# Feature attentions: maxima and values leave their PSUM bank through ScalarE, one subtraction on GpSimd, a bias folded into another

## The chip, the cores and the metric

The kernel runs on one core of one Trainium2 chip. The metric is the device time of one execution in microseconds (us), the median of several runs. PE is the matrix engine (PEld its weight loads), DVE the vector engine, ACT the scalar engine, POOL GpSimd, SP the engine that issues most DMAs; "ACTq" and "SPq" in a timeline are DMA issues of those engines' queues.

## What is computed

A chain of eight residual blocks on x (32 x 64 x 256) with a context of the same size; between them stand layer norms. The blocks are called A to H in the kernel. The change touches the two "feature attentions", A and E, in which the positions of the attention are the 256 features and the 64 rows of a sample are split in heads of 8:

```python
# A: q = layernorm(x), k = v = ctx, each (32, 64, 256): 8 heads of 8 rows, 256 queries and keys
qk = jnp.einsum('bhdq,bhdl->bhql', qh, kh) * scale
sm = jax.nn.softmax(qk, axis=-1)
ret = jnp.einsum('bhql,bhdl->bhdq', sm, vh)
x = x + gamma * ret

# E: the same on layernorm(x) with projections over the 64 rows and a band of +-64 features
qkv = x @ w_in.T + b_in
q, k, v = jnp.split(qkv, 3, axis=-1)
scores = jnp.where(band, q @ k / sqrt(8), -inf)
attn = jax.nn.softmax(scores, axis=-1)
o = attn @ v
o = o @ w_out.T + b_out
out = (relu(o).T * ctx) projected by w_ct, + b_ct
```

B, D, F and H are feed-forward blocks (D with an attention of its own and experts, H with experts), C an attention over tokens, G an attention with a sigmoid.

## The kernel before

The 2048 rows are 16 tiles of 128 rows (two samples each). Stages A to H run one after the other; each stage loads the next one's weights. In A and E all 16 tiles go through one software pipeline, `attention_slots`, in which the order of every instruction is written out by hand: time is cut in slots t, a tile takes eight slots, and tile i meets its steps at fixed offsets from 8i. Steps of several tiles share a slot. The steps, with their offsets:

- `prepare` (-2 to 9): layer norm, q (in E the projections, L1139 and L1141: qp and kp on PE, fq and fk on ACT), then `stacks`: q and k are each split on POOL into three bfloat16 terms (t3q, t3k: L194 to L198), written to DRAM by SP (d3q, d3k) and loaded again as stacked rows (stq, stk, 192 KB each, L211).
- `score_maxima` (16 to 26): 16 score products of a tile (L242; in E with the band added first, L238), two a slot; DVE takes the negated maxima (negm, L246). At offset 24 PE transposes them (nmT, L250); they too are split in three bfloat16 terms: the first on ACT (nm, L253), the remainder on DVE (nmr, L256), the second and third on POOL (L257, L258). At offset 26 three DMAs of ACT's queue (L261) put the terms as three more rows into stq, so that the scores of the next step come out with the maximum taken off.
- `values` (23): transposed values in PSUM (cT in A, vp in E, L1165), copied by DVE into vmo (L441; in E L1168, where the values' bias is added).
- `attend_unit` (30 to 37): score products with the keys on partitions (L273), exponent on ACT (e, L277), in E the band cut out by POOL (L285).
- `product_unit` (32 to 39): values times exponents into o (L295), two slots after their unit.
- `finish` (40 to 52): oc copied from o by ACT (L356), the denominators by two products (den, L306), copied by ACT (rd, L308), reciprocals on DVE (L312), num, and in E two more projections (o2 at L1178, o3 at L1185; y on ACT adds b_out at L1180).

In slot 24 of a tile PE does: the first half of a unit's scores (L273), one score product of the next tile (L242), nmT, the second half (L273), the product o, the second L242; slot 25 begins with den of the tile before. DVE's order there is negm, the two vmo copies, negm, negm, nmr, ACT's is e, oc, nm, e, rd, e, the three DMA issues, and in E fq.

Each engine runs its instructions in the order in which they were written. The PSUM tiles cT, vp, nmT, den, qp, kp, o2 and o3 carry the tag "tp", for which there is one buffer: whoever comes next in PE's order waits until the last reader of the one before is done. For nmT that last reader is nmr on DVE (it reads `src`, the transposed maxima), for cT and vp the second vmo copy. The score tiles s1 and s2 and the work pools have two buffers each, o has one, e four.

`load_E` issues the DMAs of E's weights during stage D; `first_of_E` runs E's constants and the first tiles' operands beside D's last products.

Of the kernel before, what the change touches and what calls it, by code (L numbers as in the profile page):

```python
# [9 lines left out]
F32 = mybir.dt.float32  # L10
# [3 lines left out]
ALU = mybir.AluOpType  # L14
# [3 lines left out]
P = 128  # L18
T = 2048
D = 256  # L20
# [11 lines left out]
def tile_net(ctx: ExitStack, tc: tile.TileContext, a: dict, out: bass.AP):  # L32
    nc = tc.nc
    V, S, G, PE = nc.vector, nc.scalar, nc.gpsimd, nc.tensor
# [9 lines left out]
    def fetch(i):  # L44
        nc.sync.dma_start(xs[i], a["x"][i * P : (i + 1) * P, :])
        nc.sync.dma_start(cs[i], a["ctx_2048"][i * P : (i + 1) * P, :])
# [53 lines left out]
    def bcast_row(pool, src, n, name):  # L100
        t = pool.tile([P, n], F32, name=name)
        nc.sync.dma_start(t, src.partition_broadcast(P) if len(src.shape) == 1 else src.to_broadcast([P, n]))
        return t
# [78 lines left out]
    def values_of(vmo, lc):  # L182

        return vmo[:, lc].rearrange("p c (q z) -> p c q z", z=40)[:, :, :, 0:8]
# [38 lines left out]
    def banded(band):  # L223
        return [(0, 192), (64, 256)] if band is not None else [(0, D), (0, D)]

    def score_maxima(pool, psum, k, qs, ks, band, i):

        qr = banded(band)
        negm = pool.tile([P, 2, 16], F32, name="negm")
        for qc in range(2):
            lo, hi = qr[qc]
            for hp in range(8):
                sc = psum.tile([P, 2, D], F32, tag="s1", name=f"s1_{i}_{qc}_{hp}", bufs=2)
                if band is not None:
                    PE.matmul(  # L238
                        sc[:, :, lo:hi], identb, band[:, qc, :, lo:hi], start=True, stop=False, skip_group_check=True,
                    )  # L240
                for hh in range(2):
                    PE.matmul(  # L242
                        sc[:, hh, lo:hi], qs[0:96, 2 * hp + hh, qc * P : (qc + 1) * P], ks[0:96, 2 * hp + hh, lo:hi],
                        start=band is None, stop=True, skip_group_check=band is not None,
                    )
                V.tensor_reduce(negm[:, qc, 2 * hp : 2 * hp + 2], sc[:, :, lo:hi], AX.X, ALU.max, negate=True)  # L246
                yield
        tp = psum.tile([P, 2, P], F32, tag="tp", name=f"nmT_{i}")
        for qc in range(2):
            PE.transpose(tp[0:16, qc, :], negm[:, qc, :], ident)  # L250
        src = tp[0:16].rearrange("h c t -> h (c t)")
        nm3 = pool.tile([16, 3, D], BF, name="nm3")
        S.copy(nm3[:, 0, :], src)  # L253
        yield
        r = pool.tile([16, D], F32, name="nmr")
        V.tensor_tensor(r, src, nm3[:, 0, :], ALU.subtract)  # L256
        G.tensor_copy(nm3[:, 1, :], r)  # L257
        G.tensor_tensor(nm3[:, 2, :], r, nm3[:, 1, :], ALU.subtract)  # L258
        yield
        for t in range(3):  # L260
            nc.scalar.dma_start(qs[96 + t : 97 + t], nm3[:, t, :])  # L261
        yield
# [139 lines left out]
    def run_A(w, side):  # L402
        with ExitStack() as es:
            cp = es.enter_context(tc.tile_pool(name="Ac", bufs=1, side=side))
            pool = es.enter_context(tc.tile_pool(name="Aw", bufs=2, side=side))
            dram = es.enter_context(tc.tile_pool(name="Ad", bufs=4, space=bass.MemoryType.DRAM))
            psum = es.enter_context(tc.tile_pool(name="Ap", bufs=1, space=PSUM))
            k = {}
            parts = attention_constants(cp, k)
            masks = []  # L410

            def prepare(i):
                if i + AHEAD < NT:
                    fetch(i + AHEAD)
                if i == 3:
                    pending.pop()()
                mv, rstd = ln_stats(pool, [xs[i]])
                V.tensor_scalar(mv[:, :, 0], mv[:, :, 0], -1.0, None, ALU.mult)
                yield
                q = pool.tile([P, D], F32, name="q")  # L420
                G.tensor_scalar(q, xs[i], mv[:, 0, 0:1], rstd, ALU.add, ALU.mult)
                if i < 4:
                    operand_buffers(cp, k, i)
                yield
                yield
                yield
                yield from stacks(pool, k, dram, q, cs[i], i)

            def start(t):
                if t in (16, 18):  # L430
                    next(parts)
                if t == 20:
                    for r in range(2):
                        masks.append(cp.tile([P, 1], F32, name=f"gmask{r}"))
                        V.tensor_tensor(masks[r], k["mask"][r], w["gamma"], ALU.mult)

            def values(i):
                tp = transpose_to(psum, cs[i], "tp", f"cT_{i}")
                yield
                for lc in range(2):  # L440
                    V.tensor_copy(  # L441
                        values_of(k["vmo"][i % 2], lc), tp[:, lc, :].rearrange("p (c q d) -> p c q d", c=4, q=4)
                    )
                yield

            def finish(i, oc):

                rd = yield from normalised(pool, psum, k, oc, i, 4, masks)
                G.tensor_tensor(xs[i], xs[i], rd, ALU.add)
                yield  # L450

            attention_slots(pool, psum, k, None, SCALE8, prepare, values, finish, start)


# [633 lines left out]
    def load_E(wp):  # L1088
        w = {}
        w["band"] = load(wp, [P, 2, D], a["c_band"], "band")  # L1090
        for nm in ("b_in", "b_out", "b_ct"):
            w[nm] = load(wp, [P, 3 if nm == "b_in" else 1], a[f"L2_xattn_{nm}"], nm)
        w["bv"] = bcast_row(wp, a["L2_xattn_bv"], P, "ebv")
        bd = wp.tile([P, 5, P], F32, name="bd")
        G.memset(bd, 0.0)
        for h0 in (0, 64):
            rows = slice(h0, h0 + 64)
            nc.sync.dma_start(
                bd[rows, 0:3, h0 : h0 + 64], a["L2_xattn_w_in"].rearrange("i (t o) -> i t o", t=3)
            )  # L1100
            nc.sync.dma_start(bd[rows, 3, h0 : h0 + 64], a["L2_xattn_w_out"])
            nc.sync.dma_start(bd[rows, 4, h0 : h0 + 64], a["L2_xattn_w_ct"])
        w["bd"] = bd

        between.append(lambda psum: first_of_E(w, psum))
        return w
# [3 lines left out]
    def first_of_E(w, psum):  # L1110

        w["k"], w["cstack"], w["normed"] = {}, ExitStack(), {}
        side = side_of("E")
        cp = w["cstack"].enter_context(tc.tile_pool(name="Ec", bufs=1, side=side))
        for b in range(4):
            operand_buffers(cp, w["k"], b)
            yield
        yield from attention_constants(cp, w["k"])
        w["bandb"] = cp.tile([P, 2, 2, D], BF, name="bandb")
        V.tensor_copy(w["bandb"], bc(w["band"], 2, [P, 2, 2, D]))  # L1120
        w["dram"] = w["cstack"].enter_context(tc.tile_pool(name="Ed", bufs=4, space=bass.MemoryType.DRAM))
        yield
        xp = w["cstack"].enter_context(tc.tile_pool(name="Ex", bufs=4, side=side))
        w["xp"] = xp
        yield
        with tc.tile_pool(name="Ef", bufs=1, side=side) as pool:
            for i in range(EARLY):
                yield from operands_of_E(w, pool, psum, i)
# [17 lines left out]
    def run_E(w, side):  # L1146
        bd = w["bd"]
        with ExitStack() as es:
# [5 lines left out]
            pool = es.enter_context(tc.tile_pool(name="Ew", bufs=2, side=side))  # L1154
            psum = es.enter_context(tc.tile_pool(name="Ep", bufs=1, space=PSUM))
            k, band, st = w["k"], w["bandb"], w["normed"]
# [4 lines left out]
            def values(i):  # L1161
                xn = st[i]
                vp = psum.tile([P, 2, P], F32, tag="tp", name=f"vp_{i}")
                for lc in range(2):
                    PE.matmul(vp[:, lc, :], xn[:, lc * P : (lc + 1) * P], bd[:, 2, :], start=True, stop=True)  # L1165
                yield
                for lc in range(2):
                    V.tensor_tensor(  # L1168
                        values_of(k["vmo"][i % 2], lc), vp[:, lc, :].rearrange("p (c q d) -> p c q d", c=4, q=4),
                        w["bv"].rearrange("p (c q d) -> p c q d", c=4, q=4), ALU.add,  # L1170
                    )
                yield

            def finish(i, oc):
# [472 lines left out]
```

## Time and profile before

| | us |
|---|---|
| median of 3 runs | 2920.18 |
| the runs | 2913.55 to 2922.21 |
| the profiled execution | 2917.11 |
| its span, first to last instruction | 2915.4 |

| engine | busy us | share |
|---|---|---|
| PE | 2455.6 | 84% |
| DVE | 1932.7 | 66% |
| ACT | 1513.6 | 52% |
| POOL | 1485.2 | 51% |

The mean granted TensorE clock was 0.962. Stage A ends at about 325 us, stage E stands between about 2057 and 2380 us. Durations of single instructions of the steps concerned (median, ns): vmo copy 281 in A and in E, nm on ACT 362, nmr on DVE 402, the second and third term on POOL 387 and 660, oc 580, rd 372.

How to read the lines below: a timeline line has start and length in us, the engine, the line of the kernel, the instruction, what it writes <- what it reads, the shape and the count of merged instructions; in brackets the idle time of the engine just before it and what ended it. A line of waits has the waiting engine and tile, the one waited for, us in total, times, and the longest.

### The profile page before, as it was taken

What the parts mean: (1) busy time and instruction counts of PE and PEld (TensorE: products, weight loads), DVE (VectorE), ACT (ScalarE), POOL (GpSimd) and SP (SyncE); (2) the same over time, 40 slices, a digit from 0 to 9 for tenths busy, and PEclk for the clock granted to TensorE, in tenths of its full rate; (3) what the DMA queues carried; (4) which work ended last, traced back from release to release, by engine and by line L of the source; (5) the groups of instructions that cost most, each with busy time, mean ns of one, the idle gap of its engine ahead of it and who ended that gap; (6) DMA issues with size and microseconds to landing.
All of it is one profiled execution on the core that took longest, in us unless ns stands there. A gap on an engine that the chain in (4) does not pass through costs nothing.

```text
span 2915.4 us, 44332 instructions
## 1 busy us (share of the span) xinstructions
PE 2455.6 (84%) x15966; PEld 1452.3 (50%) x16070; DVE 1932.7 (66%) x4084; ACT 1513.6 (52%) x2049; POOL 1485.2 (51%) x1649
## 2 busy tenths in 40 slices
PE   4888698777777777679999999789888876789999
PEld 2444344344444444446666666556555533445555
DVE  7777655599999999765545555663667659843322
ACT  1555421399999999745555555353244446521111
POOL 4554433388888888765555555311577754400000
PEclk9999899899999999989999999889999988899999
DMA  6543000399999999920000000000433300200000
GB/s 165 116 105 88 23 1 1 60 203 202 198 206 203 202 202 202 203 65 8 15 15 15 8 1 1 29 30 24 107 88 87 90 2 1 75 1 8 8 4 11
DMA packets 610744, 223.77 MB, mean 77 GB/s; under 512 B 547382, under 2 KB 600668, under 8 KB 605916
## 3 DMA queue, kind: packets, MB, share of 16 engines
q1 hardware_dynamic: 607452, 220.14, 34.6%
q8 instruction: 127, 2.08, 0.3%
q10 hardware_dynamic: 3072, 0.79, 0.2%
q14 instruction: 93, 0.76, 0.1%
HBM read 66.98 MB, written 18.87 MB: 29 GB/s over the span
## 4 chain that ended last, share of the span: by engine, by line
PE 51%; DVE 23%; issue 9%; POOL 3%; ACT 2%; DMA 1%; ACTq 0%; DVEq 0%; POOLq 0%; SPq 0%
DVE e L790 11%; PE yp L986 4%; PE vp L915 3%; PE ppq L927 3%; PE ppk L927 3%; PE hout L1503 3%; PE pgate L1524 3%; PE pup L1524 3%; PE sp L945 2%; PE ep L1073 2%; PE op L971 2%; PE hmp L1066 2%; DVE negm L246 2%; PE o L295 1%; PE sc L760 1%
## 5 line engine op out<-in xcount | busy, mean ns | idle before, releaser
L814 ACT ACTIVATE ei<-e,nb,sq 128x2048 int16<-128x2048 f32 x256 | 535.4, 2092 | 43.6 <-DVE nb L811 39.3
L824 POOL CAST eb<-ei 128x2048 bf16<-128x2048 int16 x256 | 482.5, 1895 | 116.2 <-ACT ei L814 96.9
L760 PE MATMUL sc<-kT,qz 128*128 128x512 bf16 x930 | 281.6, 382 | 154.9 <-DVE e L790 150.1
L246 DVE TENSOR_REDUCE negm<-s 128x2 f32<-128x512 f32 (+1 forms) x512 | 302.7, 610 | 148.8 <-PE s L242 146.1
L790 DVE TENSOR_SCALAR_CACHE_REDUCE e<-sc,mx 128x1024 f32<-128x1024 f32 x256 | 326.2, 1274 | 0.7 <-DVE nb L811 0.3
L790 DVE TENSOR_SCALAR_CACHE_REDUCE e<-sc 128x1024 f32<-128x1024 f32 x256 | 312.4, 1220 | 10.5 <-PE sc L760 10.5
L277 ACT ACTIVATE e<-s 128x1024 f32<-128x1024 f32 (+1 forms) x256 | 234.2, 916 | 149.2 <-PE s L273 116.8
L242 PE MATMUL s<-stk,stq 96*128 96x256 bf16 (+1 forms) x1024 | 192.3, 271 | 40.8 <-DMA d3k<-t3k 24.5
L760 PEld LDWEIGHTS <-qz 128*128 128x128 bf16 x1024 | 94.8, 97 | 260.8 <-issue 202.5
L935 POOL TENSOR_TENSOR rwq<-rwq,sin 128x512 f32<-128x512 f32 x64 | 81.1, 1268 | 240.3 <-ACT rwq L932 212.2
L273 PE MATMUL s<-stq,stk 128*128 128x256 bf16 (+1 forms) x1024 | 181.4, 263 | 8.3 <-DMA stq<-nm 5.0
L773 PEld LDWEIGHTS <-vz 128*64 128x64 bf16 x4096 | 122.6, 109 | 114.7 <-issue 113.9
L87 POOL TENSOR_TENSOR rstd<-ve,mhalf 128x1 f32<-128x1 f32 (+1 forms) x56 | 42.4, 757 | 255.0 <-DVE ve L85 148.8
L947 DVE TENSOR_REDUCE mx<-sp 128x4 f32<-128x512 f32 x64 | 44.3, 692 | 192.7 <-PE sp L945 192.7
L773 PE MATMUL av<-eT,vz 128*64 128x128 bf16 x4096 | 163.0, 222 | 10.4 <-DMA eT<-eb 7.9
L1534 DVE TENSOR_TENSOR hm<-pup,sl 128x512 f32<-128x512 f32 (+1 forms) x56 | 38.7, 691 | 191.1 <-PE pup L1524 182.5
L932 ACT ACTIVATE rwq<-ppq,dbq 64x512 f32<-64x512 f32 x128 | 87.4, 683 | 148.9 <-DVE rtq L929 148.1
L285 POOL TENSOR_SCALAR_AFFINE_SELECT e<-e 128x256 f32<-128x256 f32 (+1 forms) x256 | 133.3, 548 | 52.9 <-ACT e L277 52.8
L242 PEld LDWEIGHTS <-stq 96*128 96x128 bf16 x1024 | 94.1, 101 | 131.5 <-issue 108.9
L295 PE MATMUL o<-e,vmo 128*32 128x256 f32 (+1 forms) x2048 | 150.5, 366 | 3.8 <-POOL e L285 2.0
L1532 ACT ACTIVATE sl<-pgate 128x512 f32<-128x512 f32 (+1 forms) x56 | 33.4, 597 | 219.4 <-PE pgate L1524 219.4
L915 PE MATMUL vp<-Dwv,hnT 128*128 128x512 f32 x256 | 123.9, 606 | 4.0 <-ACT hnT L890 4.0
(345 smaller groups left out, 5493.3 us busy)
## 6 DMA issues: line engine op xcount, KB each, us to landing
stk<-d3k SPq DMA_DIRECT2D x96, 192.0 KB
stq<-d3q SPq DMA_DIRECT2D x96, 192.0 KB
d3k<-t3k SPq DMA_DIRECT2D x160, 64.0 KB
d3q<-t3q SPq DMA_DIRECT2D x96, 64.0 KB
eT<-eb SPq DMA_TRANSPOSE x256
fw<-in_L_ffn_w SPq DMA_DIRECT2D x3, 1024.0 KB
x<-in_x SPq DMA_DIRECT2D x16, 128.0 KB
c<-in_ctx SPq DMA_DIRECT2D x16, 128.0 KB
```

The costliest lines, as they stand in the source:

```text
L242: PE.matmul(sc[:, hh, lo:hi], qs[0:96, 2 * hp + hh, qc * P : (qc + 1) * P], ks[0:96, 2 * hp + hh, lo:hi], start=band is None, stop=True, s ...
L246: V.tensor_reduce(negm[:, qc, 2 * hp : 2 * hp + 2], sc[:, :, lo:hi], AX.X, ALU.max, negate=True)
L273: PE.matmul(sc[:, c, lo:hi], ks[:, h, lc * P : (lc + 1) * P], qs[:, h, lo:hi], start=True, stop=True)
L277: S.activation(e[:, :, lo:hi], sc[:, :, lo:hi], AF.Exp, scale=scale)
L295: PE.matmul(o[32 * c : 32 * c + 32, q // 2, lo:hi], vmo[:, lc, c, 32 * q : 32 * q + 32], e[:, c, lo:hi], start=u == 0, stop=q % 2 == 1 and ...
L760: PE.matmul(sc[:, k0 : k0 + 512], qz[i % 2][:, h, :], kT[:, h // 2, 1024 * part + k0 : 1024 * part + k0 + 512], start=True, stop=True,)
L773: PE.matmul(av[i][r0 : r0 + 64, h // 4, :], vz[:, kt, h // 4, h % 4, :], eT[:, kt, :], start=h == 0 and kt < 2, stop=h == H - 1 and kt >= ...
L790: V.tensor_scalar(e, scs.pop((n, part)), 1.0, mx[:, 0:1] if part else LOWEST, ALU.mult, ALU.max, accum_out=mx[:, part : part + 1],)
L814: S.activation(ei, es_.pop(n), AF.Exp, bias=nb, scale=sq[i][:, h : h + 1], accum_out=sums[i][:, h : h + 1],)
L824: G.tensor_copy(eb, eis.pop(n - 1))
L915: PE.matmul(vp, hnT[g][:, c, j * P : (j + 1) * P], wv[:, c, :], start=c == 0, stop=c == 1)
L927: PE.matmul(pp, wt[:, c, hh * P : (hh + 1) * P], hnT[g][:, c, :], start=c == 0, stop=c == 1)
```

## The change

Three edits in the two stages, and a constant.

1. `score_maxima`: ACT copies the transposed maxima to SBUF in float32 (`r`, the tile nmr) and then takes the first bfloat16 term from PSUM; the remainder, `r` minus the first term, is computed on GpSimd from SBUF instead of on DVE from PSUM.
2. `values` of A: ACT instead of DVE copies cT into vmo.
3. `values` of E: ACT instead of DVE copies vp into vmo, and no bias is added there. In its place `first_of_E` multiplies the values' bias by w_out (`bd[:, 3, :]`) and adds the product to b_out; the DMA that spread the bias over the partitions is gone from `load_E`.

```diff
@@ score_maxima
         nm3 = pool.tile([16, 3, D], BF, name="nm3")
+        r = pool.tile([16, D], F32, name="nmr")
+        S.copy(r, src)
         S.copy(nm3[:, 0, :], src)
         yield
-        r = pool.tile([16, D], F32, name="nmr")
-        V.tensor_tensor(r, src, nm3[:, 0, :], ALU.subtract)
+        G.tensor_tensor(r, r, nm3[:, 0, :], ALU.subtract)
         G.tensor_copy(nm3[:, 1, :], r)
         G.tensor_tensor(nm3[:, 2, :], r, nm3[:, 1, :], ALU.subtract)
@@ run_A, values
                 for lc in range(2):
-                    V.tensor_copy(
-                        values_of(k["vmo"][i % 2], lc), tp[:, lc, :].rearrange("p (c q d) -> p c q d", c=4, q=4)
-                    )
+                    S.copy(values_of(k["vmo"][i % 2], lc), tp[:, lc, :].rearrange("p (c q d) -> p c q d", c=4, q=4))
@@ load_E
-        w["bv"] = bcast_row(wp, a["L2_xattn_bv"], P, "ebv")
@@ first_of_E
         yield from attention_constants(cp, w["k"])
+
+        bp = psum.tile([P, 1], F32, tag="tp", name="ebout")
+        PE.matmul(bp, w["bd"][:, 3, :], w["b_in"][:, 2:3], start=True, stop=True)
+        V.tensor_tensor(w["b_out"], w["b_out"], bp, ALU.add)
@@ run_E, values
                 for lc in range(2):
-                    V.tensor_tensor(
-                        values_of(k["vmo"][i % 2], lc), vp[:, lc, :].rearrange("p (c q d) -> p c q d", c=4, q=4),
-                        w["bv"].rearrange("p (c q d) -> p c q d", c=4, q=4), ALU.add,
-                    )
+                    S.copy(values_of(k["vmo"][i % 2], lc), vp[:, lc, :].rearrange("p (c q d) -> p c q d", c=4, q=4))
```

In the order of each engine, ACT then has in slots 23 to 26: e, the two vmo copies, oc, nmr's copy, nm, e, rd, e, the DMA issues. POOL has the new nmr right before the second term, and DVE loses three instructions a tile. PE's and SP's orders are the same but for the one product added and the one DMA removed.

## The prediction

> **What bounds the kernel now.** The page first: PE is busy 84% of the span, and the feature attentions (stage A, about 40 to 320 us, and stage E, about 2060 to 2375 us) are the slices that the change touches. The table of windows then gives each engine's load in the steady part of the two stages (columns: length, then busy us and instructions of PE, weight loads, DVE, ACT and POOL, the granted clock, the DMA share, GB/s):
>
> ```profile
> 195.00:230.00 35.00, 27.88 (x267) 15.16 (x260) 25.46 (x54) 18.49 (x22) 18.00 (x33) 0.99 0.44 100
> 2200.00:2240.00 40.00, 33.70 (x331) 21.00 (x327) 28.39 (x60) 18.40 (x29) 30.54 (x60) 1.00 0.37 88
> ```
>
> PE leads in both, but with holes; ACT is half idle, POOL is half idle in A and three quarters full in E. Which waits make PE's holes is in the list of waits, first of A (20 to 320 us), then of E (2060 to 2375 us): who waited for whom, us in total, times, longest.
>
> ```profile
> PE den L306 <- DVE nmr L256: 15.7, 14, 1.2
> PE nmT L250 <- DVE vmo L441: 11.5, 16, 1.1
> PE s L273 <- DMA stq<-nm: 5.0, 7, 1.6
> ...
> PE den L306 <- DVE nmr L256: 14.1, 14, 1.1
> PE nmT L250 <- DVE vmo L1168: 9.2, 16, 1.0
> ```
>
> The first two of each stage are what the change removes: 15.7+11.5+14.1+9.2 = 50.5 us of PE idling on DVE because cT/vp, nmT and den take turns in the one PSUM buffer "tp". The third line is what may come instead: the maxima's terms must land in stq before the attention of a tile starts. The timeline of one A tile shows the turn (start, us, engine, line):
>
> ```profile
> 212.69 1.02 ACT L277 ACTIVATE e<-s 128x1024 f32<-128x1024 f32 x1 [0.75 <-PE s L273]
> 214.13 0.48 DVE L441 COPY vmo<-cT 128x128 f32<-128x128 f32 x2
> 214.67 0.39 PE L250 MATMUL nmT<-ident,negm 128*16 128x128 f32 x2 [0.74 <-DVE vmo L441]
> 216.81 0.40 DVE L256 TENSOR_TENSOR nmr<-nmT,nm 16x256 f32<-16x256 f32 x1
> 217.36 1.10 PE L306 MATMUL den<-oc,shift 128*128 128x256 f32 x4 [1.19 <-DVE nmr L256]
> ```
>
> nmr itself is queued on DVE behind a reduction. And the same turn of an E tile, with what comes after it on POOL and ACT:
>
> ```profile
> 2199.11 0.39 PE L250 MATMUL nmT<-ident,negm 128*16 128x128 f32 x2 [0.55 <-DVE vmo L1168]
> 2200.80 1.96 POOL L285 TENSOR_SCALAR_AFFINE_SELECT e<-e 128x512 f32<-128x512 f32 x4
> 2201.62 1.10 PE L306 MATMUL den<-oc,shift 128*128 128x256 f32 x4 [1.06 <-DVE nmr L256]
> 2202.71 0.39 POOL L257 CAST nm<-nmr 16x256 bf16<-16x256 f32 x1
> 2203.18 0.66 POOL L258 TENSOR_TENSOR nm<-nmr,nm 16x256 bf16<-16x256 f32 x1
> 2203.58 1.80 ACTq L261 DMA_DIRECT2D stq<-nm  x3
> 2205.43 0.47 ACT L1141 ACTIVATE fq<-qp,b_in 128x256 f32<-128x256 f32 x1 [1.12 <-PE s L273]
> 2206.14 0.62 PE L1139 MATMUL kp<-xn,bd 128*128 128x256 f32 x2
> ```
>
> In E POOL has no gap before nm (it runs from 2196.4 to 2203.84), so nm waits for POOL, not for nmr. One early E tile (nmT at 2085.17) shows what happens when the third term is late:
>
> ```profile
> 2089.30 0.66 POOL L258 TENSOR_TENSOR nm<-nmr,nm 16x256 bf16<-16x256 f32 x1
> 2091.25 0.47 ACT L1141 ACTIVATE fq<-qp,b_in 128x256 f32<-128x256 f32 x1 [2.90 <-DMA stq<-nm]
> 2091.78 0.70 PE L1139 MATMUL kp<-xn,bd 128*128 128x256 f32 x2 [0.80 <-ACT fq L1141]
> ```
>
> ACT's third DMA waits for POOL, fq waits behind it, kp waits for fq's buffer, and PE loses 0.80 us.
>
> [...] The trace has 362 (nm), 372 (rd) and 580 (oc)[...]. [...] in A the rows need some 6 us after their last issue (issue from 167.57 for 1.79 us, PE released at 175.19). [...]
>
> **The change part by part.** *(1) vmo copies to ACT.* In A they move from DVE (2 x 0.28) to ACT behind e: 213.71 to 214.21. nmT also needs the tile's last maxima, done on DVE at about 214.21. So nmT starts near 214.28 instead of 214.67: 0.39 gained, not the 0.74 of the wait. E: e ends 2198.09, vmo near 2198.6, last maximum at 2198.66: nmT near 2198.70, 0.41 gained. Behind the copies on ACT stands oc, moved from 213.61 to 214.22-214.80; the product that overwrites o follows nmT by 0.53, so PE waits at most 0.06 more.
>
> *(2) ACT empties nmT.* Two ACT copies of 0.36 follow oc: in A 214.80 to 215.52, in E 2199.18 to 2199.9. PE reaches den at about 215.83 and 2200.2, so the whole den wait goes: 217.36 becomes 215.83 (1.53 with part 1), 2201.62 becomes 2200.21 (1.41). The next e starts 0.1 later on ACT; its product is two slots (3 us) away, which hides it.
>
> *(3) nmr on GpSimd.* Not in this trace on that engine. The nearest row, L258, has the same shape and operands: 0.66, plus 0.08 between dependent POOL instructions, 0.74. Below: nothing, were it hidden in a gap[...]. I take 0.74. In A POOL has finished q at 216.99 and then needs 1.9 for three instructions: nm is whole at 218.88, against 218.41. ACT's DMAs do not stand at that point but behind e of the next slot, which moves with PE from 219.30 to 217.77; the third is issued near 220 instead of ending at 221.09. So the landing moves up by about 1.0 of the 1.5, PE's wait on stq grows by 0.5. Gain of an A tile: 1.0. Bounds: 0.39, if the landing stays where the stk/stq loads (issued from 217.18, unmoved) put it; 1.53, if it follows fully. Thirteen tiles have den and nmT: 13 us; the first two and the last have part 1 alone: 1.2. Together 14.
>
> In E POOL's chain has no gap, so nm is whole at 2204.58 instead of 2203.84, while PE now comes 1.41 earlier. The third DMA can start at 2204.62. fq then follows after 0.65 (one issue of 0.6, a third of the three above) or 1.29 (the 2085 tile, where SP issues at the same time), kp 0.53 after fq: 2205.80 to 2206.40, against 2206.14. So of 1.41 between 0.34 and -0.26 is left; SP's three stq issues should be over by then, so I take 0.2. Ten tiles (nmT 2120 to 2296): 2 us. The three last (2315, 2333, 2352) have no kp behind them: 1.4+1.4+0.75. The 2102 tile keeps about 0.75, the 2085 tile loses 0.74. Together 5.6.
>
> *(4) The bias.* Attention weights sum to one, so w_out times the values' bias can go to b_out. Adds one 128x1 product and one 128x1 addition in stage D (DVE's ve, 128x1, is 0.154); removes one SP issue (0.43, at 1243.6, used at 2071). All beside D's expert products: nothing, at worst 0.4.
>
> *(5) DVE* loses 2 x 0.28 + 0.40 = 0.96 a tile. It is not the leader; in A's first tiles, where it is, 0.5 at most.
>
> Sum: 14 + 5.6 = 19.6, say 20. The profiled execution took 2917.1 (span 2915.4 and 1.7 around it), 3.1 below the median of the three runs, 2920.2: 2897 from the one, 2900 from the other. I forecast 2898. What stands between and behind the stages (PE-bound B to D, F to H) is shifted whole: A's end starts stage B's POOL memset of 13.75 us, which moves with it.
>
> **Rivals.** *All of it:* the landing follows and POOL finds room: 13 x 1.53 + 1.2 in A, 13 x 1.41 + 1.2 in E, 41 us: 2876. For it: POOL idles 6 to 7 us a tile in A. Against: the 2085 tile. *Hardly anything:* in A only the 0.39 of 15 tiles, in E nothing: 2911. For it: PE already waits for the landing in 7 tiles of A, whose loads do not move. *Slower, by the third term in E:* the subtraction takes 1.1 on GpSimd and fq follows by 1.29: nm whole at 2205.02, kp at 2206.84, 0.7 later than now, in 12 tiles 8.4, with no gain in A: 2925. It decides from where nm is whole later than 2204.32 (with 1.29) or 2204.96 (with 0.65). *The change doing something else:* no; the instruction order moves just these.
>
> **How the numbers follow.** Forecast 0.60 (2886 to 2908, by A's bounds of about 7 either way and E's 0.34 to -0.26), all of it 0.14, hardly anything 0.15, slower 0.11. 0.3% (8.8 us, about what a measurement of this kernel can tell from no change) puts "faster" below 2911.4: 0.60 + 0.14 and a small part of the third case, 0.76; same 0.13; slower 0.11. The range 2878 to 2914 leaves out the slow case and half of "all of it".
>
> **What would show it.** Right: no den wait on nmr; nmT's wait down to about 0.3 and put down to DVE's negm or ACT; in E kp waiting about 1 us for fq and fq behind the stq DMA; in A the wait on stq at 1 us in most tiles. Wrong: a period of an A tile still near 16.9 us, or of an E tile over 19.3; a GpSimd nmr far from 0.66[...].

## The result, and the profile after

| | before | after |
|---|---|---|
| median, us | 2917.36 | 2879.01 |
| lowest to highest, us | 2913.55 to 2922.21 | 2875.77 to 2881.86 |
| the profiled execution, us | 2917.11 | 2879.53 |
| mean granted TensorE clock | 0.962 | 0.962 |

The ratio is 0.9869, its 95% interval 0.9853 to 0.9884: 38 us faster, where 20 were forecast. The time lies inside the range, by 1 us at its lower end, and next to the rival "all of it". The tables of medians leave out one run, of the experiment "bias alone", that took 4085.11 us at a granted clock of 0.562. In the profiled executions stage A (first nmT to last nmT) went from 255.3 to 232.3 us, E from 280.1 to 268.3: 23.0 and 11.9 of the 37.6 us. The remaining 2.7 lie ahead of, between and behind these two stretches.

The same windows as before, in the kernel after (columns as there):

```profile
195.00:230.00 35.00, 31.66 (x309) 17.17 (x304) 28.27 (x55) 21.71 (x31) 20.57 (x37) 1.00 0.50 114
2200.00:2240.00 40.00, 35.53 (x354) 21.99 (x352) 28.82 (x57) 19.91 (x36) 32.49 (x63) 1.00 0.39 93
```

PE's busy share rose from 80% to 90% of the A window, but only from 84% to 89% of the E window. The lists of waits of the kernel after, first A (20 to 320 us), then PE's own list of E (2035 to 2345 us, because the stage now starts earlier):

```profile
PE s L274 <- DMA stq<-nm: 5.4, 7, 1.8
...
PE s L274 <- issue: 2.3, 1, 2.3
PE s L274 <- DMA d3k<-t3k: 2.3, 1, 2.3
...
PE nmT L250 <- ACT vmo L442: 2.2, 10, 0.5
...
PE kp L1141 <- ACT fq L1143: 11.8, 13, 1.3
...
PE nmT L250 <- ACT vmo L1170: 0.2, 1, 0.2
```

den no longer waits for nmr in either stage, and nmT's wait is nearly gone. The wait on stq in A is about what it was (5.0 us in 7 waits before), but two more waits of 2.3 us stand at the same product, the first one of the attention: all of PE's waits there, those for e included, sum to 10.3 us, where they were 7.2. In E a new line leads: kp waits for fq in 13 tiles, 11.8 us. One A tile of the kernel after (timeline, PE weight loads left out):

```profile
137.11 0.43 ACT L442 COPY vmo<-cT 128x128 f32<-128x128 f32 x2
...
137.59 0.46 PE L250 MATMUL nmT<-ident,negm 128*16 128x128 f32 x2 [0.17 <-ACT vmo L442]
...
138.08 0.36 ACT L254 COPY nmr<-nmT 16x256 f32<-16x256 f32 x1
...
139.00 1.03 PE L307 MATMUL den<-oc,shift 128*128 128x256 f32 x4
...
140.46 0.66 POOL L257 TENSOR_TENSOR nmr<-nmr,nm 16x256 f32<-16x256 f32 x1
...
140.86 2.00 ACTq L262 DMA_DIRECT2D stq<-nm  x3
...
141.66 0.66 POOL L259 TENSOR_TENSOR nm<-nmr,nm 16x256 bf16<-16x256 f32 x1
...
148.18 0.38 PE L274 MATMUL s<-stq,stk 128*128 128x256 bf16 x2 [0.39 <-DMA stq<-nm]
```

den follows nmT after 1.41 us (2.69 in the tile shown of before). ACT's three issues begin 3.27 after nmT, the third waits for the term that POOL ends at 142.32, and all end at 142.86. PE is released at 148.18. (This is one of the shorter waits of the stage.) An E tile of the kernel after, from vmo to kp:

```profile
2208.18 0.43 ACT L1170 COPY vmo<-vp 128x128 f32<-128x128 f32 x2
...
2208.66 0.52 PE L250 MATMUL nmT<-ident,negm 128*16 128x128 f32 x2
...
2210.08 1.05 PE L307 MATMUL den<-oc,shift 128*128 128x256 f32 x4
...
2211.99 3.33 ACTq L262 DMA_DIRECT2D stq<-nm  x3
...
2212.93 0.66 POOL L257 TENSOR_TENSOR nmr<-nmr,nm 16x256 f32<-16x256 f32 x1
...
2214.12 0.66 POOL L259 TENSOR_TENSOR nm<-nmr,nm 16x256 bf16<-16x256 f32 x1
...
2215.38 0.47 ACT L1143 ACTIVATE fq<-qp,b_in 128x256 f32<-128x256 f32 x1 [2.65 <-DMA stq<-nm]
...
2215.90 0.70 PE L1141 MATMUL kp<-xn,bd 128*128 128x256 f32 x2 [0.85 <-ACT fq L1143]
```

This is the 2085 tile of the kernel before, now in 13 tiles: the third issue stands on ACT until POOL is done (2214.78), fq behind it, kp behind fq.

### The profile page after: what moved, and what is told of

Read it like the earlier page. It is cut to its first block, busy times and chain, and to the rows that moved or that the text cites. A ratio compares the mean times of both kernels' runs of the same rounds, so it can differ in the third digit from the quotient of the medians.

```text
span 2877.8 us, 44432 instructions
## 1 busy us (share of the span) xinstructions
PE 2468.2 (86%) x16072; PEld 1449.1 (50%) x16072; DVE 1914.5 (67%) x3989; ACT 1531.7 (53%) x2145; POOL 1506.4 (52%) x1681
## 4 chain that ended last, share of the span: by engine, by line
PE 50%; DVE 22%; issue 9%; POOL 5%; ACT 2%; DMA 1%; ACTq 0%; DVEq 0%; POOLq 0%; SPq 0%
DVE e L789 11%; PE yp L985 4%; PE ppq L926 3%; PE ppk L926 3%; PE hout L1502 3%; PE vp L914 3%; PE pgate L1523 3%; PE pup L1523 3%; PE sp L944 2%; PE ep L1072 2%; PE op L970 2%; PE hmp L1065 2%; PE sc L759 1%; PE op L495 1%; POOL e L286 1%
## 5 line engine op out<-in xcount | busy, mean ns | idle before, releaser
L759 PE MATMUL sc<-kT,qz 128*128 128x512 bf16 x1024 | 298.1, 382 | 142.0 <-DVE e L789 139.9
```

The lines of the kernel that those rows point to most:

```text
L759: PE.matmul(sc[:, k0 : k0 + 512], qz[i % 2][:, h, :], kT[:, h // 2, 1024 * part + k0 : 1024 * part + k0 + 512], start=True, stop=True,)
```

## The experiments

The reading to test was: PE's turn on the bank "tp" had cost an A tile and an E tile nearly the same; an A tile now gets all of it unless it must wait for stq, and E gives most of it back, because fq stands behind an issue that waits for GpSimd. The rivals were that E is bound by something else (POOL's own load, nearly full), and that in A the landing of the rows depends on the large loads and not on the issue.

| run | median us | ratio to before | 95% interval |
|---|---|---|---|
| after | 2879.01 | 0.9869 | 0.9853 to 0.9884 |
| values only | 2896.59 | 0.9927 | 0.9910 to 0.9943 |
| maxima only | 2886.6 | 0.9895 | 0.9880 to 0.9910 |
| fq first | 2864.27 | 0.9819 | 0.9804 to 0.9834 |
| subtraction on VectorE | 2866.86 | 0.9827 | 0.9811 to 0.9844 |
| subtraction twice | 2903.51 | 0.9953 | 0.9937 to 0.9969 |
| issue later in A | 2899.56 | 0.9940 | 0.9925 to 0.9955 |
| VectorE and fq first | 2859.09 | 0.9800 | 0.9785 to 0.9814 |
| VectorE in A, fq first in E | 2855.98 | 0.9788 | 0.9771 to 0.9805 |
| bias alone | 2919.44 | 1.0004 | 0.9992 to 1.0016 |

**Each half alone.** The first run takes the changed kernel with the maxima as before:

```diff
-        r = pool.tile([16, D], F32, name="nmr")
-        S.copy(r, src)
         S.copy(nm3[:, 0, :], src)
         yield
-        G.tensor_tensor(r, r, nm3[:, 0, :], ALU.subtract)
+        r = pool.tile([16, D], F32, name="nmr")
+        V.tensor_tensor(r, src, nm3[:, 0, :], ALU.subtract)
```

> The values go through ScalarE and the bias is folded, the maxima's remainder stays on VectorE. Theory (each wait is worth what the trace shows for it): nmT's wait in PE goes (0.57 us a tile in A, 0.55 in E), the den wait on nmr stays at 1.2 and 1.06; with 31 tiles and some given back at the landing in A, 8 to 16 us faster than before. Rival (the two edits only work together, because nmr's wait swallows what nmT gains): less than 4 us.

The second is the kernel before with the same lines the other way round, vmo and its bias left on VectorE.

> Only the maxima: ScalarE copies them, GpSimd subtracts; the values stay on VectorE with their bias. Theory: the den wait goes in both stages, in A it is gain (1.2 to 1.3 us in 13 tiles, the landing follows), in E nearly all of it turns into the wait of kp for fq, as GpSimd delivers the third term 0.74 us later; A's tile 15.5 us, E's 19.2 to 19.5, 16 to 24 us faster than before. Rival (E gains too): E's tile under 18.6 us and over 30 us faster.

They gain 20.5 and 30.5 us, both more than expected (the 30.5 is even what the rival of the second run said, though its E tile is not), and 51 together where the whole change gains 38. PE's list of waits of the maxima alone (2050 to 2350 us) shows one place where they stop adding up:

```profile
PE nmT L250 <- DVE vmo L1169: 9.2, 16, 1.0
PE kp L1140 <- ACT fq L1142: 9.0, 12, 1.1
```

With the maxima alone kp already waits for fq; with the values alone den still waits (14.1 us in 14 tiles, as before), and kp waits in two tiles. The lengths of a tile, read in the timeline from one nmT to the next, make it exact for the steady tiles. The columns are A tiles in which no wait on stq fell, E tiles with a kp behind them, and the last E tiles, which have no fq and kp:

| us | A, no stq wait | E, with kp | E, without kp |
|---|---|---|---|
| before | 16.06 | 19.30 | 17.67 |
| values only | 15.56 | 18.79 | 17.17 |
| maxima only | 14.63 | 18.94 | 16.40 |
| after | 14.13 | 18.95 | 15.90 |

In the first and third column the halves add up: 0.50 + 1.43 = 1.93 in A, 0.50 + 1.27 = 1.77 in E without kp. In the middle one they gain 0.51 and 0.36, and 0.35 together. This points at kp, but it does not yet rule out POOL's load: the last tiles have the same three maxima instructions on POOL, but not the splits of fq and fk, and POOL is busy 71% of such a tile and 80% of one with kp. The next run separates the two.

As whole stages the halves add up in neither: from first to last nmT of the profiled executions A lost 10.1 us with the values alone, 23.4 with the maxima alone and 23.0 with both, E 11.4, 10.0 and 11.9. In A PE's waits at the attention's first product sum to 6.8 and 6.2 us in the two halves and to 10.3 with both, and stretches of a lower granted clock (last section) fall differently in each.

**fq ahead of the issue.** In E the issue of the three rows moves to the end of the slot's list, behind the projections:

```diff
-                for kind, offset in (("m", 26), ("m", 25), ("f", 41), ("p", 2), ("p", 3), ("f", 46), ("f", 52)):
+                for kind, offset in (
+                    (("m", 26), ("m", 25), ("f", 41), ("p", 2), ("p", 3), ("f", 46), ("f", 52)) if band is None else
+                    (("m", 25), ("f", 41), ("p", 2), ("p", 3), ("f", 46), ("f", 52), ("m", 26))
+                ):
```

> The changed kernel, but in E the three DMA issues of the maxima's terms stand behind fq in ScalarE's order, in the same slot. Theory (in E kp waits for fq, fq for the third DMA issue, that for GpSimd): kp's wait of 0.86 us goes, E's tile from 18.95 to 18.1 us, in all 8 to 10 us faster than the changed kernel, near 2870. Rival (GpSimd's band masks set E's pace, and kp's wait only shows it): another wait takes its place, E's tile stays at 18.8 or more, within 3 us of the changed kernel.

It is 14.7 us faster than the change, more than expected. The timeline of an E tile of this kernel:

```profile
2112.36 0.66 POOL L257 TENSOR_TENSOR nmr<-nmr,nm 16x256 f32<-16x256 f32 x1
2112.96 0.47 ACT L1146 ACTIVATE fq<-qp,b_in 128x256 f32<-128x256 f32 x1 [0.80 <-PE qp L1144]
2113.02 1.79 ACTq L262 DMA_DIRECT2D stq<-nm  x3
...
2113.55 0.66 POOL L259 TENSOR_TENSOR nm<-nmr,nm 16x256 bf16<-16x256 f32 x1
...
2114.32 0.62 PE L1144 MATMUL kp<-xn,bd 128*128 128x256 f32 x2
```

fq now waits for its product and not for a DMA, kp for nothing. The E tile is 17.51 us, which is 1.79 below before: the 1.77 of the tiles without kp has arrived in full. POOL has as much to do as in the changed kernel (15.2 us a tile in both), so its load did not set E's pace: the rival falls. The first row's issue begins 1.6 later after nmT than in the changed kernel (4.92 against 3.33), but the last one ends at the same time (6.71 against 6.66), because it waits for POOL in both. What waits behind the issues now is e, and no PE wait follows from it:

```profile
2114.86 0.81 ACT L278 ACTIVATE e<-s 128x768 f32<-128x768 f32 x1 [1.43 <-DMA stq<-nm]
```

In the steady E tiles no wait on stq appears. The first two tiles and one of the last pay for the new order with three such waits, 3.9 us in all, the longest 3.0; in E of the changed kernel there is none. I had counted kp's wait alone (0.85 a tile); PE's waits further on, for negm and for rd, also shrank by 0.1 and 0.2, and PE's own busy time by 0.2 a tile.

**Less and more work for GpSimd.** In the one run the subtraction takes ACT's copy on VectorE:

```diff
-        G.tensor_tensor(r, r, nm3[:, 0, :], ALU.subtract)
+        V.tensor_tensor(r, r, nm3[:, 0, :], ALU.subtract)
```

> The changed kernel, but the subtraction from ScalarE's copy is on VectorE instead of GpSimd. Theory (what counts is that ScalarE frees the PSUM buffer; GpSimd's 0.74 us only makes the third term later): E's tile loses most of kp's wait, 18.95 to 18.2 us, A's stays or gains 0.2, in all 6 to 11 us faster than the changed kernel. Rival (VectorE's queue holds the subtraction back, or its two SBUF inputs disturb GpSimd): no gain or a loss of up to 8 us.

In the other GpSimd does the subtraction twice, the first time into a tile that nobody reads:

```diff
+        r2 = pool.tile([16, D], F32, name="nmr2")
+        G.tensor_tensor(r2, r, nm3[:, 0, :], ALU.subtract)
         G.tensor_tensor(r, r, nm3[:, 0, :], ALU.subtract)
```

> The changed kernel with the subtraction done twice on GpSimd (the first result is not used): 0.74 us more in front of the second and third term of every tile. Theory: in E each tile with a kp behind it becomes 0.7 us longer (18.95 to 19.7), 8 to 9 us; in A the third DMA is issued 0.5 to 0.7 us later and the landing follows, 4 to 8 us; together 12 to 17 us slower than the changed kernel. Rival for A (the landing is tied to the end of the stk and stq loads): A unchanged, 8 to 9 us slower.

12 us faster than the change, just above what was expected, and 24.5 us slower, well above it. An E tile takes 18.39 and 19.66 instead of 18.95. The steps for one GpSimd instruction of 0.66 (0.74 with its gap) are thus 0.56 and 0.71; why the first is the smaller shows below. In the run with two, the timeline of an E tile shows the sum of the chain:

```profile
2129.28 0.66 POOL L258 TENSOR_TENSOR nmr<-nmr,nm 16x256 f32<-16x256 f32 x1
2130.02 0.66 POOL L259 TENSOR_TENSOR nmr<-nmr,nm 16x256 f32<-16x256 f32 x1
...
2131.21 0.66 POOL L261 TENSOR_TENSOR nm<-nmr,nm 16x256 bf16<-16x256 f32 x1
2132.45 0.47 ACT L1145 ACTIVATE fq<-qp,b_in 128x256 f32<-128x256 f32 x1 [3.37 <-DMA stq<-nm]
...
2132.98 0.70 PE L1143 MATMUL kp<-xn,bd 128*128 128x256 f32 x2 [1.57 <-ACT fq L1145]
```

kp's wait has grown from 0.85 to 1.57, by 0.72, which is the instruction. In A the run with two has most tiles at 15.5 to 15.9 with a stq wait of 1.0 to 1.4, the run on VectorE most at 14.1 to 14.7, seven of them with none. So GpSimd's chain reaches PE in A too, by the third issue, which waits for it there as well: a steady A tile is some 0.9 longer than in the change. The time alone overstates the price of the instruction. In the profiled executions A is 3.0 us longer, E 15.3 and the rest of the span, where nothing was changed, 5.7. Of E's 15.3 some 4 lie in four tiles of 20.5 to 21.1, in each of which the granted clock falls below 0.6 for some us, and 4 in the first tile, where it does so too. (From 2110 to 2250 us it is 0.98 on the mean, and 1.00 in the changed kernel.)

**The issue alone, in A.** Here the terms are ready as in the changed kernel, but in A ACT issues the three DMAs one slot later:

```diff
-                for kind, offset in (("m", 26), ("m", 25), ("f", 41), ("p", 2), ("p", 3), ("f", 46), ("f", 52)):
+                for kind, offset in (
+                    ("m", 26 if band is not None else 27), ("m", 25), ("f", 41), ("p", 2), ("p", 3), ("f", 46), ("f", 52)):
```

> The changed kernel, but in A the three DMA issues of the terms come one slot (1.5 us) later. Theory (the landing follows the issue): PE's wait on stq grows by 1.2 to 1.5 us a tile, A's tile from 14.7 to about 16 us, 15 to 20 us slower than the changed kernel. Rival (the landing is tied to the end of the stk and stq loads, which do not move): the wait grows by less than 0.4 us a tile, at most 5 us slower.

20.5 us slower than the change, at the upper end of what was expected. From the timeline of an A tile whose nmT starts at 161.07:

```profile
165.14 0.66 POOL L259 TENSOR_TENSOR nm<-nmr,nm 16x256 bf16<-16x256 f32 x1
165.90 1.80 ACTq L262 DMA_DIRECT2D stq<-nm  x3
...
173.20 0.38 PE L274 MATMUL s<-stq,stk 128*128 128x256 bf16 x2 [1.93 <-DMA stq<-nm]
```

The terms are whole at 165.80, the issues end at 167.70 (6.63 after nmT, against 5.27 in the tile of the change shown above), and PE's wait grows from 0.39 to 1.93. Over the whole of A the waits on stq are 21.8 us in 12 tiles; all waits at that product in the changed kernel were 10.3. That is about 1.0 a tile for an issue that ends 1.35 later, so the rows follow their issue for the most part, and the rival, with its 0.4 a tile, falls. The rest of the 20.5 us is not the landing itself: six A tiles hold a stretch of a lower granted clock, in the changed kernel two. (The stretches show in the timeline as pairs of score products of about 0.6 us where others take 0.38; in the kernel before such pairs, of 0.61 to 0.64, stand at 229.81 to 232.85, where the granted clock is 0.50 from 230 to 232.)

**Both repairs.** First VectorE and fq first in both stages:

> The changed kernel with both the subtraction on VectorE and fq ahead of the DMA issues in E. Theory (both take away the same wait of kp): little more than the better of the two alone, E's tile 18.0 to 18.2 us, 8 to 12 us faster than the changed kernel. Rival (GpSimd's load in E is a bound of its own): the two add up, E's tile under 17.8 us.

2859.09 us, 5 us less than with fq first alone, and with E tiles of 17.70. Both are below what was expected. The tile is even under the rival's 17.8, but that does not speak for the rival, since fq first alone stands at 17.51: in E the second edit costs 0.19. The gain is A's (221.0 us from first to last nmT, 227.2 with fq first alone). Where the 0.19 comes from is in the timelines, first of fq first, then of this run:

```profile
2110.44 1.96 POOL L286 TENSOR_SCALAR_AFFINE_SELECT e<-e 128x512 f32<-128x512 f32 x4
2111.49 0.53 PE L296 MATMUL o<-e,vmo 128*32 128x192 f32 x8 [0.26 <-POOL e L286]
...
2196.61 0.57 DVE L257 TENSOR_TENSOR nmr<-nmr,nm 16x256 f32<-16x256 f32 x1
2196.86 2.14 POOL L286 TENSOR_SCALAR_AFFINE_SELECT e<-e 128x512 f32<-128x512 f32 x4
2198.10 0.53 PE L296 MATMUL o<-e,vmo 128*32 128x192 f32 x8 [0.45 <-POOL e L286]
```

While VectorE subtracts, GpSimd's band masks take 2.14 instead of 1.96 (the first of the four 0.82 instead of 0.64), and PE's product o waits 0.45 instead of 0.26. The subtraction itself takes 0.57 there, where it takes 0.40 in other tiles. In the E tile of before that the prediction shows, VectorE's subtraction reads one operand from PSUM and takes 0.40, and the masks beside it take 1.96. This is what the rival of "subtraction on VectorE" had in mind, and it is the missing part of that run's 0.56: 0.74 less 0.18. So the last version puts the subtraction on VectorE in A only:

```diff
-        V.tensor_tensor(r, r, nm3[:, 0, :], ALU.subtract)
+        (V if band is None else G).tensor_tensor(r, r, nm3[:, 0, :], ALU.subtract)
```

> The changed kernel with the subtraction on VectorE in A and on GpSimd in E, and in E the issue of the terms behind fq. Theory (A is set by when the third term is whole, E by what stands between PE and kp, and with fq ahead of the issue GpSimd's load costs E nothing while VectorE's does): an A tile at 14.1 us where no wait on stq falls, as with the subtraction on VectorE (14.13), an E tile at 17.5 as with fq first alone (17.51) and not 17.7, so ten tiles times 0.19 = 2 us less than with both edits everywhere: 2857. Rival (the 0.19 of E were paid by something other than where the subtraction runs): E tile 17.7 and 2859 again.

2855.98 us, E tiles of 17.50, most A tiles 14.1 to 14.3. The traces tell the two versions apart, the times don't: their intervals overlap. It is the fastest version measured, 23 us below the change. The two windows in it:

```profile
195.00:230.00 35.00, 34.78 (x339) 19.25 (x338) 31.17 (x62) 24.04 (x33) 24.64 (x46) 1.00 0.52 122
2200.00:2240.00 40.00, 37.19 (x370) 23.53 (x366) 30.08 (x63) 20.80 (x37) 34.13 (x66) 1.00 0.41 97
```

PE is busy 99% and 93% of them: in the steady part of A there is little left to take from waits.

**The bias alone.** The kernel before with the fold and a plain copy on VectorE:

```diff
-                    V.tensor_tensor(
-                        values_of(k["vmo"][i % 2], lc), vp[:, lc, :].rearrange("p (c q d) -> p c q d", c=4, q=4),
-                        w["bv"].rearrange("p (c q d) -> p c q d", c=4, q=4), ALU.add,
-                    )
+                    V.tensor_copy(
+                        values_of(k["vmo"][i % 2], lc), vp[:, lc, :].rearrange("p (c q d) -> p c q d", c=4, q=4)
+                    )
```

> The kernel before with only the bias of the values folded into that of the projection; VectorE still copies vmo, without the addition. Theory (the fold itself is worth nothing, it only makes a copy possible on ScalarE): the time of before within 3 us, an E tile still at 19.3. Rival (the addition was a cost, since nmT waits for vmo): each vmo instruction gets shorter and an E tile loses up to 0.2 us, 3 us in all, or the added product in D costs up to 0.4 us.

Ratio 1.0004, interval 0.9992 to 1.0016. PE's list of waits of E (2060 to 2375 us) is that of before:

```profile
PE den L306 <- DVE nmr L256: 14.1, 14, 1.1
...
PE nmT L250 <- DVE vmo L1171: 9.2, 16, 1.0
```

The addition took VectorE 281 ns, the copy 282. The fold by itself buys nothing; it leaves a plain copy, which the change then gives to ScalarE.

## Why the prediction was right, and too small

By its own steps:

- *(1) vmo to ACT.* The pair took 0.43 (268 ns for one). The prediction gives the pair 0.50 (213.71 to 214.21); a straight line through two ACT instructions of its trace, nm with 362 ns for 256 elements and oc with 580 for 512, puts one of 128 at 253 ns, an estimate, and two at 0.51. "nmT also needs the tile's last maxima" was half true: nmT is two transposes, and only the second one reads the maxima of the last unit. So nmT's wait fell by 0.57 in A and 0.55 in E, where 0.39 and 0.41 were priced.
- *(2) The den wait* went wholly, as said. den follows nmT earlier by 1.28 in A and 1.09 in E.
- *(3) nmr on GpSimd* takes 0.662, as L258 said. In A two terms of the sum were mis-sized. The turn at "tp", priced at 1.53 a tile, gave 0.57 at nmT and 1.28 at den, 1.85 together; tiles that don't wait ahead of the attention became 1.93 shorter. And "the landing moves up by about 1.0 of the 1.5, PE's wait on stq grows by 0.5" took off too much. Its own lines gave more: the issues begin at 217.77, and three of 1.79 in all then end at 219.56, 1.53 earlier than before; writing "near 220" lost half a microsecond. Measured against the tile's neighbours the issues ended 1.72 earlier (0.57 with nmT, 1.15 after it), and PE's waits ahead of the attention grew from 7.2 to 10.3 us over the stage, some 0.3 a tile, very unevenly: 0.69 in the tile of before with nmT at 162.94, 0.39 in the tile shown of after, 2.3 in two others. So the eleven tiles from the fourth nmT on took 1.63 us less each on the mean (1.93 less 0.3) instead of 1.0, which is beyond the bound of 1.53 "if it follows fully". (Both kernels have some 5 us of low clock in these tiles, by my estimate from what they exceed 16.06 and 14.13 plus their waits.) That stq waits 1 us "in most tiles" was wrong with it: it was so in four.
- *E.* The mechanism is the one forecast, step by step: nm later because POOL has no gap, the third issue late, fq behind it, kp waiting about 1 us. fq came 0.60 after nm was whole, so the shorter of the two cases (0.65) holds, not the 1.29 of the 2085 tile. The tile kept 0.35 of 1.77; "I take 0.2" was low by 0.15, and the bound 0.34 was reached. The 2085 tile lost 0.65 (0.74 forecast).
- *The rest of E's 11.9* against the 5.6 of the sum: two tiles of the kernel before, 20.91 and 19.37 long, hold a stretch with a lower granted clock (1.6 over 19.30 and 1.7 over 17.67) that has no like in the changed kernel's E; they make 3.3 of it. The first E tile gained 1.2 that I had not priced.
- *(4) and (5)* can't be seen in the time; for (4) the fold alone shows it, within some 5 us.

So the sum was 19.6 for 37.6: A is 9 of the missing 18 us, E 6.3, the stretches outside 2.7. That the time still fell inside the range is in part luck: the lower end, 2878, stands 1 us below the median, the four runs spread over 6 us, and one of them lies outside. The rival "all of it" came near in time (2876) but not by its reason: in E POOL found no room, and only a fifth of a tile's gain remained. The rival "slower, by the third term in E" had the right place and the wrong price: its 1.1 us for the subtraction was a guess that no trace showed (it took 0.66); nm is whole 6.12 after nmT, kp 7.24, against 7.03 before, so the wait that was added gives back 0.2 of the 0.55 that nmT had gained.

## What to carry to other kernels

When a wait for a shared buffer is removed, look in each engine's order for the next instruction that cannot move with it; if a DMA issue whose data come late stands ahead of work that another engine waits for, put the work first: here a change of order alone was worth another 15 us. Read a stage's tiles apart by what stands behind them: tiles that lack a step (here the last ones of E) show where to look, but they can lack more than one thing, so move the step alone before you believe it. Moving a small instruction to another engine can lengthen what runs beside it (here GpSimd's masks, 2.14 us instead of 1.96): with fq first, the subtraction was better on VectorE in A and worse there in E. Price a wait by what the instruction itself reads, not by what its group reads: the first transpose did not need the last maxima.

## What the runs showed of the hardware

**Order on ACT and DVE.** The pair of E timelines shows what ACT's order costs: the same fq waits 2.65 us behind a DMA issue, the last 1.85 of them with its operand ready, and put ahead of the issue 0.80, on its product. On DVE the E tile of before shows the same:

```profile
2199.53 0.36 ACT L253 CAST nm<-nmT 16x256 bf16<-16x256 f32 x1 [0.96 <-PE nmT L250]
...
2200.60 0.56 DVE L246 TENSOR_REDUCE negm<-s 128x2 f32<-128x384 f32 x1 [0.75 <-PE s L242]
...
2201.07 0.40 DVE L256 TENSOR_TENSOR nmr<-nmT,nm 16x256 f32<-16x256 f32 x1
```

nmr's last operand is whole at 2199.89, but DVE stands idle until 2200.60 for the reduction written ahead of it.

**Rows and their issue.** From the end of the third issue to PE's release the A tiles shown took 5.32 us (after) and 5.50 (issue later); in the tile of before with its nmT at 162.94, 5.8; in the waiting A tiles of after it is 5.0 to 7.2. The three rows have 8 KB each. The time runs beside the stk and stq loads; what share those have in it was not tried.

**Stretches of a low clock.** Some tiles of most traces are 1.4 to 2.7 us longer than their waits explain. The windows of the kernel before around one of its long E tiles:

```profile
2333.00:2337.00 4.00, 2.94 (x19) 1.92 (x20) 1.24 (x3) 1.06 (x2) 2.01 (x5) 0.81 0.01 2
2337.00:2341.00 4.00, 4.00 (x37) 2.23 (x36) 1.78 (x4) 1.38 (x3) 1.01 (x2) 0.76 0.03 6
2341.00:2345.00 4.00, 4.00 (x44) 2.65 (x43) 3.94 (x8) 2.23 (x3) 2.06 (x5) 1.00 0.03 6
```

and of the kernel after in A:

```profile
164.00:168.00 4.00, 3.22 (x19) 1.65 (x20) 1.62 (x6) 1.02 (x1) 0.60 (x2) 0.52 0.33 80
168.00:172.00 4.00, 3.82 (x24) 1.84 (x23) 2.12 (x4) 1.84 (x4) 3.76 (x7) 0.62 0.06 16
```

The granted clock falls to 0.5 to 0.8 in these windows of 4 us (in windows of 2 us it reaches 0.50) and comes back within some 8 us. The stretches shown begin at a pause of PE of 1 us or more (den's wait at 2335.46, a gap of 2.3 ahead of 164.78). From 60 us to the end of A there are three such stretches in the kernel before, two in the kernel after and six with the issue later, all beginning at a wait of 1.2 to 2.7 us, and none in the last two versions, whose longest wait there is 1.0. But most pauses of that length are followed by none; whether the waits set them off, and what else does, stays open. They fall in different tiles of different runs: the same A code took 232.3 us in the profile of the change and 227.2 in that of fq first. Single stages of single profiles are therefore not told apart below some 5 us; steady tiles are, to 0.1.
